# Attention and a depthwise convolution on one core: half of the last pair divided by way of DRAM, six taps moved from TensorE to VectorE

## The chip, the cores and the metric

The kernel runs on one NeuronCore of a Trainium2 chip. The metric is device time in microseconds (us) of one execution; lower is better. The time before is the median of four runs, 2910.03 us (2908.95 to 2911.59).

The engines are called by their roles: TensorE (PE in the profile) multiplies matrices, VectorE (DVE) does elementwise work, ScalarE (ACT) does activations and copies out of PSUM, GpSimd (POOL) here mostly issues DMAs, and SyncE (SP) issues DMAs only. Each engine runs its own instructions strictly in the order in which they were written.

## The reference

The input x has 16 images of 384 channels and 32 x 32 pixels, in float32. Two layers follow, each with a residual:

```python
# layer 0: attention over the 1024 pixels, 8 heads of 48 channels
x = x + _L0_conv_ref(_gn(x), L0_conv_w_qkv, L0_conv_w_proj, L0_conv_b_proj)
# layer 1: 7x7 depthwise convolution, one symmetrised filter for each channel
x = x + _L1_conv_ref(_gn(x), L1_conv_weight)
```

`_gn` is a group normalisation over 32 groups of 12 channels. Inside the attention, softmax(q k / sqrt(48)) v is computed for each head and then projected. In the convolution each output pixel is a sum over 49 taps (dy, dx), each of them one weight per channel times the shifted image.

## The kernel before, in words

Channels lie on the partitions: an image is three tiles of 128 channels x 1024 pixels. Below, "image 15" is the last of the images 0 to 15, and "tile (14, 2)" is the third channel tile of image 14.

**Attention.** The eight heads of an image are worked on as four pairs, numbered u = 4b + p. The work of a pair has two halves of 512 query columns; each half is one group of eight steps. In a group TensorE first makes eight blocks of scores (`s_step`, L493), ScalarE exponentiates them (L501), and TensorE then multiplies by v into one PSUM accumulator (`av_step`, L509). ScalarE copies the accumulator into the half `h` of `os_[u]` (`take`, L520). One extra column of v is all ones, so row 48 (and 112 for the second head) of `os_[u]` holds the sum of the exponentials, by which the rest has to be divided.

**Division by way of DRAM.** For all pairs but the last, SP copies the two rows of sums to DRAM (L527) and reads them back spread over 128 partitions (L528); VectorE takes 128 x 16 reciprocals (L534); SP writes them to DRAM (L536) and reads them back broadcast over 64 partitions for each head (L539, twice 256 KB); VectorE multiplies `os_[u]` by them (L545). These are `sums_out`, `invert` and `divide`.

**Division at once.** The last pair, u = 63, is divided half by half in `divide_at_once`: TensorE multiplies by a matrix that copies the row of sums to all rows (L588), VectorE takes the reciprocal of 128 x 512 values out of PSUM (L590) and multiplies (L591). Half 0 is divided in the last group, between its scores and its products with v; half 1 after them, in `fast_finish`. The projection of image 15 (`proj_part`, L599) runs around them: pairs 0 and 1, then pair 2, then pair 3.

**Convolution.** Most taps are one VectorE instruction each (`conv_tap`, L640): the image times a weight of its channel, added to the accumulating tile `x1s`. Taps with dx = 0 of some tiles are made on ScalarE (`product`, L621) and added by accumulating DMAs from POOL (L945). Three tiles are convolved on TensorE (`PE_TILES`): (14, 2) first, then (15, 2) and (15, 1). For them the normalised tile `xn1s` is written to DRAM (L715) and read back as shifted copies `sh` (L722, 8 DMAs of 160 KB for each half of the tile); the multiplications (`conv_on_pe`, L756) group four rows dy as one of two values d0, so that a tile has 14 products (d0, dx) for each half, of 8 instructions each. `pe_taps` (L736) leaves (1, 0) out for tile (14, 2): its dy = 1, 2, 3 with dx = 0 come from ScalarE. A half of a tile frees the buffers of its shifted copies for the next half to be loaded. The products of (14, 2) are queued in `x1_chains` and are run at the end, some of them between the small matrix products (`ps_st_x`, L332) that give the statistics of image 15.

**Order.** The program order is written by a planner in the kernel. `clock` is its estimate of TensorE's time and `vclock` of VectorE's. `after(wait, cost, f)` queues a job that is written on VectorE once `vclock` has passed the waiting time, at the cost given; `catch_up` fills VectorE with taps up to `clock`. A tap is worth about 1.0 to 1.2 us to the planner. In `x1_chains` of image 14, `vclock` is set back by 5.0 us, which leaves room for five us of taps more.

**Queues.** SP's DMAs are issued in order, and one that waits holds up all behind it: those of the division, the writes `xd` and the loads `sh`. POOL's queue holds the loads and the stores of images, the accumulating additions and the six copies (`qk_rest`, L458) that collect the last pair's q and k.

Of the kernel before, what the change touches and what calls it, by code (L numbers as in the profile page):

```python
# [10 lines left out]
F32 = mybir.dt.float32  # L11
I32 = mybir.dt.int32
AF = mybir.ActivationFunctionType
ALU = mybir.AluOpType
AX = mybir.AxisListType

P = 128
# [27 lines left out]
def kernel(  # L45
# [25 lines left out]
    nc = tc.nc  # L71

    B, C, H, W = x.shape
    N = H * W
    NK = C // P
    D = C // HEADS
    NP = HEADS // 2
    NT = N // P
    HALF = N // 2
    KS = w_conv.shape[2]  # L80
    PAD = KS // 2
    SCALE = D ** (-0.5)
    U = NP * B
    PER = C // GROUPS
    SC = 2 * N // P
# [24 lines left out]
    def run(general):  # L110
        tag = "g" if general else "f"
        with ExitStack() as stack:
# [13 lines left out]
            tpool = pool("tpool", 2)  # L126
            small = pool("small", 2)
# [16 lines left out]

            BESIDE = None if general else (B - 2, 0)
            ROWS_ONLY[BESIDE] = range(-PAD, PAD + 1)

            def taps_of(b, k):
                return [t for t in TAPS if t[1] or t[0] not in ROWS_ONLY.get((b, k), ())]
# [373 lines left out]
            def sums_out(u):  # L523
                sum_d = ddram.tile([2, N], F32, tag="sum", name=f"sum_{u}")
                for j in range(2):
                    r = 64 * j + D
                    nc.sync.dma_start(sum_d[j : j + 1, :], os_[u][r : r + 1, :])  # L527
                nc.sync.dma_start(sums[:, u, :], sum_d.rearrange("j (p c) -> (j p) c", c=SC))  # L528
# [56 lines left out]
            def divide_at_once(u, h):  # L585
                half = os_[u][:, h * HALF : (h + 1) * HALF]
                ps = ps_o.tile([P, HALF], F32, tag="acc", name=f"ps_sum_{u}_{h}")
                nc.tensor.matmul(ps, lhsT=late["masks"][:, 7, :], rhs=half, start=True, stop=True)  # L588
                inv = tpool.tile([P, N], F32, tag="t", name=f"inv_{u}_{h}")[:, 0:HALF]
                nc.vector.reciprocal(inv, ps)  # L590
                nc.vector.tensor_tensor(half, half, inv, ALU.mult)  # L591

            def proj_part(b, o, ts):
                if o not in pps:
                    pps[o] = psum(f"ps_proj_{b}_{o}")
                for t in ts:
                    lhsT = wp[:, t, o * P : (o + 1) * P] if t < NK else late["w3"][:, o * P : (o + 1) * P]
                    for h in range(2):
                        nc.tensor.matmul(  # L599
                            pps[o][:, h, :],  # L600
                            lhsT=lhsT,
                            rhs=os_[NP * b + t][:, h * HALF : (h + 1) * HALF],
                            start=(t == 0),
                            stop=(t == NP - 1),
                        )
# [128 lines left out]
            PE_TAPS.sort(key=lambda t: t[1] != 0)  # L734

            def pe_taps(b, k):  # L736
                return [t for t in PE_TAPS if t != (1, 0) or (b, k) not in ROWS_ONLY]

            def conv_on_pe(b, k, h, first, last):
                if (b, k) == PE_TILES[-1]:  # L740
# [131 lines left out]
            def after(wait, cost, f):  # L872

                nonlocal count
                count += 1
                heapq.heappush(later, (now() + wait, count, cost, f))
# [208 lines left out]
            def x1_chains(b, st):  # L1085
                nonlocal vclock
                on_pe = [t for t in PE_TILES if t[0] == b]
                for k in range(NK - 1, -1, -1):
                    conv_begin(st, b, k, nc.vector if (b, k) == (B - 1, NK - 1) else None)
                    if (b, k) in on_pe:  # L1090
                        conv_store(b, k)

                        cuts = (0, KS - 2, KS, KS + 2) if b == B - 2 else (0, KS)
                        cuts = (*cuts, len(pe_taps(b, k)))
                        pe_conv.extend((b, k, 0, *c) for c in zip(cuts, cuts[1:]))
                        pe_conv.extend(((b, k, 1, 0, KS), (b, k, 1, KS, cuts[-1])))
                if b == B - 1:
                    lone_sums(*LONE)
                    after(2.5, 0.0, lambda: lone_rows(*LONE))
                if b == B - 2:  # L1100

                    vclock -= 5.0
                    for k in range(NK):
                        spare[B - 1, k] = new_xn1(B - 1, k)
                    beside, first = BESIDE, PE_TILES[0]
                    early = [(beside, 0), (beside, -1), (beside, 1), (first, 1), (beside, -2)]
                    early += [(first, 2), (beside, 2), (first, 3), (beside, -3), (beside, 3)]
                    for n, (bk, dy) in enumerate(early):
                        applies.append(
                            (  # L1110
                                clock + 2.0 + 7.0 * n,
                                1.3,
                                lambda n=n, bk=bk, dy=dy: rows_early(*bk, n, dy),
                            )
                        )
                after(
                    2.0 if b == B - 1 else 6.0,
                    0.0,
                    lambda: chains.extend(
                        (b, k) for k in range(NK) if (b, k) not in on_pe  # L1120
                    ),
                )
# [28 lines left out]
            waiting = set()  # L1151

            def finish(u):
                sums_out(u)
                if u < U - 1:
                    waiting.add(u)
                    after(6.0 if u % NP == NP - 1 else 9.0, 0.3, lambda: finish2(u))

# [135 lines left out]

            def fast_end(b):
                assert not applies
                for key in ("sum2", "sum3"):
                    late[key] = opool.tile([P, N], F32, tag="o", name=key)
                nc.gpsimd.memset(late["sum3"][:, N - W :], 0.0)

                x1_stats[b].groups_on_pe(late["masks"], tap, conv_piece)
                conv_piece()
                x1_chains(b, x1_stats[b])
# [7 lines left out]
            for b, n0, size in [  # L1311
# [14 lines left out]
                ending = b == B - 1 and r + size == PER_B  # L1326
                if ending:
                    catch_up(clock)
                    divide_at_once(NP * b + NP - 1, 0)
                    vclock += 4.2  # L1330
                    for o in range(NK):
                        proj_part(b, o, (0, 1))
                    loads(1)
                    clock += 2 * US_PROJ
                else:
                    catch_up(clock)
                    act_slot(4.5)
                    other(n0 + size, False)
                for n in range(n0, n0 + size):
                    av_step(n)  # L1340
                    u, h, i = n // (2 * NT), n // NT % 2, n % NT
                    if i == NT - 1:
                        take(u, h)
                clock += (size * US_STEP + US_TURN) / 2
                if n0 // (2 * NT) < (n0 + size) // (2 * NT):
                    finish((n0 + size) // (2 * NT) - 1)
                if ending:
                    catch_up(clock)
                    assert not invs and not waiting
                    fast_finish(b)  # L1350
                else:
                    other(n0 + size, True)
# [91 lines left out]
```

## Time and profile before

| what | us |
|---|---|
| median of the runs | 2910.03 |
| the profiled execution's own time | 2906.77 |
| its span, first to last instruction | 2904.6 |
| TensorE busy | 2894.6 (100%) |
| VectorE busy | 2566.1 (88%) |
| ScalarE busy | 1461.5 (50%) |
| GpSimd busy | 262.2 (9%) |

The time of an engine is counted from the span's start. In a line of the timeline, the first number is the start, the second the duration of the merged run of like instructions, then come engine, source line, operation, output and inputs, shape and the number of instructions; brackets hold the idle time of the engine before them and what ended it. SPq and POOL rows of DMAs tell when the DMA was issued, not when it landed. A matmul of float32 data shows as two instructions.

### The profile page before, as it was taken

The numbers are of one execution on the slowest core, as the hardware profiler recorded it, in microseconds if no ns is written. First come the engines' busy times: TensorE is split into PE (matmuls) and PEld (weight loads), VectorE is DVE, ScalarE is ACT, GpSimd is POOL, SyncE is SP. The second block draws the span as 40 slices with busy tenths as digits, with TensorE's granted clock in tenths as the row PEclk, the third lists the DMA queues.
The fourth block names the chain that finished last, engine by engine and source line by source line (L and its number), as shares of the span: only waits on it lengthen the run. The fifth ranks groups of instructions, "written<-read, shape, count | busy, mean of one in ns | idle before, by whom it ended". The sixth has DMA issues, their size and how long they took to land.

```text
span 2904.6 us, 30161 instructions
## 1 busy us (share of the span) xinstructions
PE 2894.6 (100%) x11446; PEld 1168.4 (40%) x11446; DVE 2566.1 (88%) x2559; ACT 1461.5 (50%) x1745; POOL 262.2 (9%) x411
## 2 busy tenths in 40 slices
PE   9999999999999999999999999999999999999999
PEld 4343343433434343343433434343343433434333
DVE  5313999989899898998989899898998989899997
ACT  3546445464453645545465454645545455454641
POOL 3111004010100101000010100101001010100101
PEclk9999999999999999999999999999999999999999
DMA  7423012220312203022120212213012130222346
GB/s 287 131 26 63 16 36 77 39 66 22 66 33 43 70 21 84 16 35 70 35 71 16 64 41 43 64 28 84 16 36 70 28 77 16 53 52 43 83 125 174
DMA packets 74284, 175.80 MB, mean 61 GB/s; under 512 B 30528, under 2 KB 32464, under 8 KB 72592
## 3 DMA queue, kind: packets, MB, share of 16 engines
q0 software_dynamic: 34336, 114.90, 15.9%
q1 hardware_dynamic: 38080, 55.20, 7.5%
q10 hardware_dynamic: 1712, 3.67, 0.4%
q8 instruction: 92, 1.51, 0.2%
q14 instruction: 64, 0.52, 0.1%
HBM read 118.61 MB, written 28.72 MB: 51 GB/s over the span
## 4 chain that ended last, share of the span: by engine, by line
PE 100%; DVE 0%; ACT 0%; POOL 0%; issue 0%; POOLq 0%
PE ps_s L493 31%; PE acc L509 31%; PE ps_qk L442 17%; PE ps_v L468 9%; PE ps_proj L562 8%; PE ps_conv L756 2%; PE ps_proj L599 1%; PE warm L1182 0%; PE ps_st_x L332 0%; PE ps_sum L588 0%; ACT qk L449 0%; POOL sc_x L353 0%; DVE x L360 0%; DVE x L777 0%; DVE ones_warm L1176 0%
## 5 line engine op out<-in xcount | busy, mean ns | idle before, releaser
L640 DVE SCALAR_TENSOR_TENSOR x<-xn,wsym,x 128x930 f32<-128x930 f32 (+9 forms) x2170 | 2362.9, 1165 | 137.2 <-ACT xn L364 137.1
L501 ACT ACTIVATE e<-ps_s 128x1024 f32<-128x1024 f32 x1024 | 952.4, 1053 | 52.4 <-PE ps_s L493 49.4
L493 PE MATMUL ps_s<-qk 48*128 48x512 f32 x4096 | 914.9, 596 | 1.1 <-ACT qk L449 1.1
L509 PE MATMUL acc<-e,v 128*64 128x512 f32 x4096 | 907.2, 595 | 0.0
L493 PEld LDWEIGHTS ps_s<-qk 48*128 48x128 f32 x4096 | 375.7, 185 | 536.5 <-ACT e L501 259.9
L509 PEld LDWEIGHTS acc<-e,v 128*64 128x64 f32 x4096 | 283.0, 137 | 608.2 <-issue 601.6
L442 PE MATMUL ps_qk<-x,wqk 128*128 128x512 f32 x1152 | 505.7, 595 | 1.0 <-DVE x L360 1.0
L520 ACT COPY o<-acc 128x512 f32<-128x512 f32 x128 | 75.0, 586 | 595.9 <-PE acc L509 595.9
L442 PEld LDWEIGHTS ps_qk<-x,wqk 128*128 128x128 f32 x1152 | 216.2, 190 | 287.1 <-issue 285.7
L468 PE MATMUL ps_v<-wv,x 128*128 128x384 f32 x768 | 252.0, 488 | 0.0
L562 PE MATMUL ps_proj<-o,wp 128*128 128x512 f32 x540 | 234.2, 592 | 0.0
L449 ACT COPY qk<-ps_qk 128x1024 f32<-128x1024 f32 x96 | 96.8, 1009 | 256.3 <-PE ps_qk L442 256.3
L577 POOL DMA_DIRECT2D x<-in_x x45 | 39.3, 872 | 1802.2 <-ACT x L570 1427.8
L468 PEld LDWEIGHTS ps_v<-wv,x 128*128 128x128 f32 x768 | 144.6, 190 | 109.7 <-ACT e L501 12.1
L562 PEld LDWEIGHTS ps_proj<-o,wp 128*128 128x128 f32 x540 | 102.6, 190 | 126.0 <-issue 119.6
L477 ACT COPY v<-ps_v 128x384 f32<-128x384 f32 x128 | 55.1, 483 | 185.6 <-PE ps_v L468 185.6
L570 ACT ACTIVATE x<-ps_proj,bp 128x1024 f32<-128x1024 f32 x45 | 50.1, 1113 | 182.7 <-PE ps_proj L562 182.7
L545 DVE TENSOR_TENSOR o<-o,inv 128x1024 f32<-128x1024 f32 x63 | 77.0, 1222 | 56.6 <-DMA inv<-inv 46.7
L364 ACT ACTIVATE xn<-x,sc_x 128x1024 f32<-128x1024 f32 x47 | 54.9, 1230 | 68.8 <-DMA sc_x<-gr_x 59.5
L387 DVE BATCH_NORM_STATS2 bs_all<-xs 128x6 f32<-128x512 f32 x84 | 52.3, 683 | 19.4 <-DMA xs<-in_x 19.2
L756 PE MATMUL ps_conv<-sh,mat 128*32 128x464 f32 (+3 forms) x656 | 67.4, 569 | 0.0
L364 ACT ACTIVATE x<-x,x_sc 128x1024 f32<-128x1024 f32 x42 | 51.1, 1263 | 22.2 <-DMA x<-in_x 22.2
(143 smaller groups left out, 560.6 us busy)
## 6 DMA issues: line engine op xcount, KB each, us to landing
x<-in_x POOLq DMA_DIRECT2D x90, 512.0 KB, 5.5
inv<-inv SPq DMA_DIRECT2D x126, 256.0 KB
out<-x POOLq DMA_DIRECT2D x45, 512.0 KB, 3.8
xs<-in_x POOLq DMA_DIRECT2D x42, 512.0 KB, 6.5
qk<-qk POOLq DMA_DIRECT2D x96, 128.0 KB, 5.9
o<-o SPq DMA_DIRECT2D x90, 64.0 KB
sh<-xd SPq DMA_DIRECT2D x32, 160.0 KB
x<-in_x SPq DMA_DIRECT2D x6, 512.0 KB
```

What stands on the lines that cost most here:

```text
L364: nc.scalar.activation(dst, src, AF.Identity, bias=self.sc[:, k, 1:2], scale=self.sc[:, k, 0:1],)
L442: nc.tensor.matmul(ps[:, h, :], lhsT=wqk[:, k, s, t, :], rhs=xns[b][:, k, h * HALF : (h + 1) * HALF], start=(k == 0), stop=(k == NK - 1),)
L449: nc.scalar.copy(halves(qks[u][:, s, :]), ps)
L468: nc.tensor.matmul(ps[:, j, 0:C], lhsT=xns[b][:, k, t * P : (t + 1) * P], rhs=wv[:, k, :], start=(k == 0), stop=(k == NK - 1),)
L493: nc.tensor.matmul(ps[:, j, :], lhsT=qks[u][r, 1, i * P : (i + 1) * P], rhs=qks[u][r, 0, h * HALF : (h + 1) * HALF], start=True, stop=True,)
L501: nc.scalar.activation(es[n], ps, AF.Exp, scale=SCALE)
L509: nc.tensor.matmul(accs[u, h][64 * j : 64 * j + 64, :], lhsT=v_of(u, i, j), rhs=e[:, j, :], start=(i == 0), stop=(i == NT - 1),)
L520: nc.scalar.copy(os_[u][:, h * HALF : (h + 1) * HALF], accs.pop((u, h)))
L545: nc.vector.tensor_tensor(os_[u], os_[u], invs.pop(u), ALU.mult)
L562: nc.tensor.matmul(ps[:, h, :], lhsT=wp[:, t, o * P : (o + 1) * P], rhs=os_[NP * b + t][:, h * HALF : (h + 1) * HALF], start=(t == 0), sto ...
L640: nc.vector.scalar_tensor_tensor(acc, xn1s[b, k].rearrange("p (h w) -> p h w", w=W)[:, iy, ix], wsym[:, k, dy + PAD, dx + PAD : dx + PAD + 1],
L756: nc.tensor.matmul(dst[CH * i : CH * (i + 1), :].rearrange("p (y x) -> p y x", x=W)[:, :, ox], lhsT=mats[k][:, i, d0 * KS + dx + PAD, :], ...
```

## The change

The change has four parts.

1. Half 0 of the last pair (u = 63) is divided by way of DRAM instead of at once. `half_sums` is called when half 0 has been taken, at the end of the group before the last; `half_invert` (128 x 8 reciprocals) is written 4.0 us later and `half_divide` 7.5 us after that. Half 1 is still divided at once. SP's six DMAs of this stand in its queue at two places: the three of `half_sums` ahead of L536 and L539 of pair 62, the three of `half_invert` behind four loads `sh` and ahead of the next four.
2. The planner's 4.2 us for the division at once are gone, and `sums_out` of the last pair, which only feeds the check of the sums, is written later, in `fast_end`.
3. For tile (14, 2), `pe_taps` leaves out (1, -1) and (1, 1) besides (1, 0): 11 products for each half are left of 13. The six taps dy = 1, 2, 3 with dx = -1 and 1 become six VectorE instructions, written together 1.0 us after `x1_chains` of image 14 (`aside`), at a planned cost of 7.0 us.
4. `vclock` is set back by 3.0 us instead of 5.0, and two of ScalarE's products change places, so that the first addition to tile (14, 2) comes one place later.

```diff
+            ASIDE = (1, -1)
...
+            def half_sums(u):
+                sum_d = ddram.tile([2, HALF], F32, tag="sumh", name=f"sumh_{u}")
+                for j in range(2):
+                    r = 64 * j + D
+                    nc.sync.dma_start(sum_d[j : j + 1, :], os_[u][r : r + 1, 0:HALF])
+                late["sumh"] = small.tile([P, SC // 2], F32, tag="sumh", name=f"sumh_{u}")
+                nc.sync.dma_start(late["sumh"], sum_d.rearrange("j (p c) -> (j p) c", c=SC // 2))
+                after(4.0, 0.3, lambda: half_invert(u))
+
+            def half_invert(u):
+                nc.vector.reciprocal(late["sumh"], late["sumh"])
+                inv_d = ddram.tile([2, HALF], F32, tag="invh", name=f"invh_{u}")
+                nc.sync.dma_start(inv_d.rearrange("j (p c) -> (j p) c", c=SC // 2), late["sumh"])
+                inv = tpool.tile([P, N], F32, tag="t", name=f"invh_{u}")[:, 0:HALF]
+                for j in range(2):
+                    nc.sync.dma_start(
+                        inv[64 * j : 64 * j + 64, :], inv_d[j : j + 1, :].to_broadcast([64, HALF])
+                    )
+                after(7.5, 0.7, lambda: half_divide(u, inv))
+
+            def half_divide(u, inv):
+                half = os_[u][:, 0:HALF]
+                nc.vector.tensor_tensor(half, half, inv, ALU.mult)
+                late["half"] = True
...
             def pe_taps(b, k):
-                return [t for t in PE_TAPS if t != (1, 0) or (b, k) not in ROWS_ONLY]
+                return [t for t in PE_TAPS if (b, k) not in ROWS_ONLY or not t[0] or t[1] not in (0, *ASIDE)]
...
-                    vclock -= 5.0
+                    vclock -= 3.0
...
+                    def aside():
+                        for dy in range(1, PAD + 1):
+                            for dx in ASIDE:
+                                conv_tap(*first, dy, dx)
+
+                    after(1.0, 7.0, aside)
-                    early = [(beside, 0), (beside, -1), (beside, 1), (first, 1), (beside, -2)]
+                    early = [(beside, 0), (beside, -1), (beside, 1), (beside, -2), (first, 1)]
...
             def finish(u):
-                sums_out(u)
                 if u < U - 1:
+                    sums_out(u)
                     waiting.add(u)
...
             def fast_end(b):
                 assert not applies
+                sums_out(U - 1)
...
                     catch_up(clock)
-                    divide_at_once(NP * b + NP - 1, 0)
-                    vclock += 4.2
                     for o in range(NK):
                         proj_part(b, o, (0, 1))
...
+                if b == B - 1 and r + 2 * size == PER_B:
+                    half_sums(n0 // (2 * NT))
...
-                    assert not invs and not waiting
+                    assert not invs and not waiting and late["half"]
```

## The prediction

> **What bounds the kernel now.** I read the page first, then the chain that ended last over the tail, then the timelines of VectorE, SP and POOL over the last 200 us, and last the trace's records of when DMAs landed.
>
> ```profile
> PE 100%; DVE 0%; ACT 0%; POOL 0%; issue 0%; POOLq 0%
> ...
> 2797.64 1.05 PE ps_sum L588 x2
> ...
> 2817.93 0.86 PE ps_sum L588 x2
> ...
> 2836.95 61.22 PE ps_conv L756 x596
> 2898.17 0.02 issue
> 2898.19 0.69 DVE x L777
> ```
>
> The chain is TensorE from end to end: what leaves it could be worth its full time. But VectorE has almost no slack. In its last 200 us, but for the small steps of image 15's statistics and the very last addition, it waits only where a bracket stands here:
>
> ```profile
> 2732.14 1.23 DVE L545 TENSOR_TENSOR o<-o,inv 128x1024 f32<-128x1024 f32 x1 [0.63 <-issue]
> ...
> 2771.95 1.23 DVE L545 TENSOR_TENSOR o<-o,inv 128x1024 f32<-128x1024 f32 x1 [2.29 <-ACT xn L621]
> ...
> 2799.50 1.22 DVE L545 TENSOR_TENSOR o<-o,inv 128x1024 f32<-128x1024 f32 x1
> 2800.63 3.35 DVE L590 RECIPROCAL inv<-ps_sum 128x512 f32<-128x512 f32 x1
> 2804.09 0.69 DVE L591 TENSOR_TENSOR o<-o,inv 128x512 f32<-128x512 f32 x1
> 2804.70 12.79 DVE L640 SCALAR_TENSOR_TENSOR x<-xn,wsym,x 128x841 f32<-128x841 f32 x12
> 2817.41 1.22 DVE L901 TENSOR_TENSOR x<-x,xn 128x1024 f32<-128x1024 f32 x1
> 2818.82 3.36 DVE L590 RECIPROCAL inv<-ps_sum 128x512 f32<-128x512 f32 x1 [0.20 <-PE ps_sum L588]
> ...
> 2891.19 1.23 DVE L918 TENSOR_TENSOR sum<-sum,sum 128x1024 f32<-128x1024 f32 x1 [1.81 <-DMA sum<-tap_-3_13772]
> ```
>
> See that VectorE reaches the second reciprocal 0.20 us before TensorE's sum is there. From it a chain runs without a gap through the residual, the statistics (the mean is ready at 2831.8, as TensorE's filling piece of convolution ends at 2831.82), the normalised tiles (2839.2), their store and the loads of shifted copies. So VectorE's lateness at 2818.82, called s below, shifts the rest of the kernel by s. The 2.29 us at 2771.95 were spent on a division's DMAs: the trace has inv<-inv of pair 61 land at 2771.42 (ScalarE, which the bracket names, has no part in this multiplication). The first two queues:
>
> ```profile
> 2711.68 0.53 POOL L651 DMA_DIRECT2D out<-x  x1 [0.45 <-DVE x L640]
> 2717.37 0.87 POOL L945 DMA_DIRECT2D xn<-xn  x1 [5.16 <-ACT xn L621]
> 2717.93 2.27 POOL L458 DMA_DIRECT2D qk<-qk  x4
> ...
> 2722.18 0.34 SPq L536 DMA_DIRECT2D inv<-rec  x1
> 2727.24 1.12 SPq L539 DMA_DIRECT2D inv<-inv  x2
> ...
> 2759.71 0.34 SPq L536 DMA_DIRECT2D inv<-rec  x1
> 2761.18 1.62 SPq L539 DMA_DIRECT2D inv<-inv  x2
> ```
>
> The same 8 KB take 1.4 us at 2759.71 and 5.0 us at 2722.18, where POOL's copies are under way (their last lands at 2727.03).
>
> **Part 1, TensorE's share.** One matmul of sums (1.05 us in the chain) and, of tile (14, 2), two products for each of two halves go. The 82 such products of the three tiles (13 x 2 and 14 x 4) take 4.25 + 1.72 + 61.22 = 67.2 us, 0.82 us each; four are 3.3 us. If all were paid: -4.35 us. Neither is paid in full.
>
> The matmul at 2797.64 is followed by a wait for VectorE's second division. Counting VectorE's new order with each tap at its step between starts in the trace (1.00 us for 841 pixels to 1.16 for 992): with 128x8 reciprocals (0.16) and one multiplication (0.61) in place of 3.46 + 0.61, but four taps (4.3) more between the two divisions and L901 (1.14) moved behind the second, VectorE reaches the second reciprocal at 2818.81 if no DMA delays it, the same instant as before. The 1.05 us become idle time: 0.
>
> The 3.3 us lie where TensorE does (14, 2) while (15, 2) is normalised, stored and loaded:
>
> ```profile
> 2836.89 15.57 PE L756 MATMUL ps_conv<-sh,mat 128*32 128x464 f32 x152
> ...
> 2842.33 11.55 SPq L722 DMA_DIRECT2D sh<-xd  x6
> ```
>
> The first loads of (15, 2) go out at 2842.33, 0.07 us after the store of that tile has landed (2842.26), and land between 2845.6 and 2850.45; TensorE came to (15, 2) at 2852.33, so 1.9 us of slack. Ready 3.3 us sooner, it would wait 1.4 us. One store of an image (out, 512 KB, issued at 2847.56) moves out of this stretch with VectorE's later taps, for which I take 0.3 us. Paid: **-2.2 us** (bounds: -1.5, were the loads slower, to -3.3, were they not awaited).
>
> **Part 2, VectorE's six taps.** Two each of 961, 930 and 899 pixels: 2 x (1.13 + 1.10 + 1.07) = 6.6 us, at 2707.3. The planner's room of 7.0 + (3.0 - 5.0) puts as many other taps behind the next reciprocals: all divisions of pairs 60, 61 and 62 keep their place in VectorE's order, +0.1 us. But the last taps of image 13 move by 6.6 us, and with them its three stores on POOL, from 2709.67-2711.68 to about 2716.3-2718.3. Behind them in POOL's queue stand the addition (2717.37) and the copies qk<-qk. The stores' data took 4.3 us before, so the copies end about 2.9 us later, at 2730. The 8 KB of pair 60 then land at 2730 instead of 2727.2, the two inv<-inv after them (4.7 us from issue to landing before) at about 2735, and VectorE, there at 2731.6, is about 3 us late. (Bounds 0.6, were the stores to drain in the shadow of the addition, to 5.)
>
> That lateness puts pair 61's reciprocal from 2759.44 to 2762.5, behind the additions and loads of POOL at 2759.47 to 2762.8, which it preceded before. Its 8 KB then take some 5 us as at 2722.18, to 2768, and inv<-inv some 6.5 (10.2 before, but most of the loads have gone by then): 2774.7 instead of 2771.42. VectorE resumes about 3.2 us late; the old 2.29 us of idle time swallow the rest. Nothing after it gives this time back: **s = +3.2 us** (bounds 0 to 5).
>
> On the DMA engines, the Trainium skill (DMA: Bandwidth & Descriptors, section Queues, rings and completion order) says that an engine goes round among the queues at the bounds of packets of some 9 to 17 descriptors. By that SP's 8 KB would wait for one packet and not for all that POOL has queued, s would be about 0 and the kernel 2 us faster. The row at 2722.18 disagrees: no packet of SP's queue moved until 2725, when POOL's had drained. I go by the row.
>
> **Part 3, the half by way of DRAM.** The half is taken at 2791.20. Sums to DRAM and back: 1.2 to 2.0 us and 1.5 us in the rows of other pairs when nothing else moves: landed at 2794.5; VectorE asks at 2797.6. But pair 62's inv<-rec is queued behind these three and goes out at 2793.4 instead of 2789.91, its inv<-inv lands at 2799.9-2800.4 (5.3 us as before, with loads sh beside it), and VectorE wants it at 2800.0: 0 to 0.5 us. Then four loads sh (1.8 us of issue), the half's inv<-rec (to 2802.3-2803.2, behind those loads), its broadcast (a 256 KB one took 3.2 to 3.7 us in quiet, at 2649; the half is 128 KB each): 2806.0-2807.0, wanted at 2805.45. Alone this makes s = 0.6 to 1.6. With part 2's 3.2 us VectorE comes at 2808.7, after them: they don't add, s is the larger of the two. If every hop were as slow as the slowest rows, the broadcast would land at 2813.8: s = 8.4.
>
> **What is moved without cost.** `sums_out` of pair 63 waits for half 1's division, about 2823, and is read by the check at 2844. ScalarE's products keep their slots; the additions that now follow each other on one tile wait for each other on POOL (4 to 5 us), with 12 us to the next. VectorE's remaining taps after the second division are 3.3 us more; its last sum starts at 2893.2 + s, free of the old wait of 1.81 us, and its last tap work ends at 2895.5 + s, TensorE at 2898.17 - 2.2 + s: 0.5 us of slack left, where before it waited 3.98 us.
>
> **Sum.** -2.2 + 0 + 3.2 = +1.0 us on the profiled execution's 2906.77 us: 2907.8. That execution is 3.3 us below the median; I add the same to the median: 2910.03 + 1.0 = **2911.0 us**.
>
> **The rivals.**
> A. The queues take up the moved stores, and only part 3's wait is left: s = 1.1, -2.2 + 1.1 = -1.1, 2908.9. For it: VectorE's order of divisions hardly moves. Against it: 2722.18, where SP's small transfer waited for POOL's.
> B. TensorE's saving comes through: 4.35 us less, 2905.7. It needs the shifted copies 1.4 us earlier and VectorE 1 us ahead, and VectorE has 0.20.
> C. Slower: SP's queue. Six small dependent transfers and four loads stand one behind another between 2791 and 2807, and VectorE, all TensorE's last projection and the statistics stand behind the last. With every hop at its slowest row s = 8.4: -2.2 + 8.4 = +6.2, 2916.2. It decides from s = 2.2 on, and exceeds 0.2% from s = 8.0. Against it: nothing of POOL's is in flight then (its last addition landed at 2787.56).
>
> **Chances.** 0.2% is 5.8 us, about what a measurement of this kernel can tell from no change. Forecast 0.52 (s from 1.5 to 5: 2909.3 to 2912.8), A 0.27, B 0.08, C 0.13. The forecast, A and B lie within 0.2%; I give faster 0.04 (half of B, were more than the counted work to go), slower 0.12 (most of C), same 0.84. The range leaves out B and the upper part of C and adds 1 us for the spread of the runs: 2907.0 to 2914.5.
>
> **What would show it.** Right: the multiplication of pair 60 starts at about 2735 and that of 61 at about 2775 after 2 to 3 us of idle time each; stores of image 13 at 2716 to 2718; TensorE idle some 4 us ahead of the last projection and 1 us ahead of (15, 2), no longer 100% of the chain; the half's multiplication without a wait. Wrong: pair 61 resumed at 2772 (then A), the half's multiplication preceded by several us of idle time (C), or a span under 2901 (B).

## The result, and the profile after

The changed kernel takes 2912.75 us (median of 40 runs, 2909.41 to 2916.03), the kernel before 2909.06 us (60 runs, 2906.34 to 2913.95). The ratio is 1.0013, with an interval from 1.0009 to 1.0018: a real loss of 3.7 us, below the 0.2% that the prediction set as its bound. The profiled execution took 2912.7 us (span 2910.9), about the median.

Ahead of everything else: which work bounds the kernel. On the page after, the shares of the chain that ended last by engine read

```profile
PE 82%; DVE 12%; DMA 3%; issue 2%; ACT 0%; POOL 0%; SPq 0%; ACTq 0%; DVEq 0%; POOLq 0%
```

where it was TensorE at 100% before. VectorE and DMAs (those of the divisions and the loads of shifted copies) are now part of what ends last. The timeline of the changed kernel shows where (columns: start in us, busy time in us, engine, line, operation; in brackets the idle time ahead of it). VectorE first, then TensorE:

```profile
2723.44 0.25 DVE L536 RECIPROCAL rec<-sums 128x16 f32<-128x16 f32 x1
...
2738.74 1.23 DVE L547 TENSOR_TENSOR o<-o,inv 128x1024 f32<-128x1024 f32 x1 [5.67 <-ACT e L503]
2777.72 1.23 DVE L547 TENSOR_TENSOR o<-o,inv 128x1024 f32<-128x1024 f32 x1 [1.80 <-issue]
...
2811.08 0.68 DVE L618 TENSOR_TENSOR o<-o,invh 128x512 f32<-128x512 f32 x1
...
2824.42 3.35 DVE L592 RECIPROCAL inv<-ps_sum 128x512 f32<-128x512 f32 x1
...
2791.16 7.14 PE L495 MATMUL ps_s<-qk 48*128 48x512 f32 x32
...
2821.85 1.02 PE L627 MATMUL ps_proj<-o,mat 128*128 128x512 f32 x2
2828.62 6.91 PE L627 MATMUL ps_proj<-o,mat 128*128 128x512 f32 x10 [5.75 <-DVE o L593]
...
2844.73 12.24 PE L784 MATMUL ps_conv<-sh,mat 128*32 128x464 f32 x120
...
2858.69 45.87 PE L784 MATMUL ps_conv<-sh,mat 128*32 128x512 f32 x444 [0.82 <-DMA sh<-xd]
```

The same two places of TensorE in the kernel before:

```profile
2790.50 7.14 PE L493 MATMUL ps_s<-qk 48*128 48x512 f32 x32
...
2822.06 5.52 PE L599 MATMUL ps_proj<-o,mat 128*128 128x512 f32 x12
```

(The brackets name what came last by the profile; what VectorE waits for at both multiplications is the inv<-inv. That of pair 60 landed at 2738.56.) The multiplications of pairs 60 and 61 come 6.6 and 5.8 us later than before, and the second reciprocal 5.6 us, without a wait for TensorE. TensorE stands idle for 5.75 us ahead of the last projection. And its ten matmuls then take 6.91 us, where twelve took 5.52 before: that was in no step of the prediction. The half's multiplication (L618) waits for nothing.

The profiled executions differ by some 3 us already ahead of the last group, as is told below ("The clock at the start"). So from here on all is counted from the start of the last group's first scores (the last 32 matmuls of L493 before, of L495 after): 2790.50 before, 2791.16 after. "Late" means later than before on that count. The rows are the start of the multiplications of pairs 60 and 61, of the second reciprocal (its lateness is s), and of the very last addition (2898.19 before, 2904.60 after; its lateness is the change in the kernel's end), and for TensorE the idle time ahead of the last projection's ten matmuls and their duration. The first column is the median less that of the kernel before on the same chip; the ratio is not the quotient of these medians. One execution of half_recips took 6200.54 us and is left out of its row.

| kernel | median | ratio, interval | 60 late | 61 late | s | idle | ten matmuls | end late |
|---|---|---|---|---|---|---|---|---|
| after | +3.7 | 1.0013, 1.0009 to 1.0018 | 5.9 | 5.1 | 4.9 | 5.75 | 6.91 | 5.8 |
| half_only | +0.9 | 1.0004, 0.9995 to 1.0013 | 0.0 | 0.0 | 1.0 | 1.83 | 4.56 | 1.1 |
| stores_later | +3.9 | 1.0012, 1.0003 to 1.0021 | 4.9 | 4.3 | 4.1 | 4.93 | 6.25 | 4.3 |
| products_later | +1.5 | 1.0005, 0.9996 to 1.0014 | 0.5 | 2.8 | 2.6 | 3.40 | 5.97 | 2.7 |
| both_later | +2.0 | 1.0004, 0.9995 to 1.0013 | 0.2 | 3.0 | 2.9 | 3.68 | 7.60 | 4.3 |
| taps_later | +1.3 | 1.0004, 0.9995 to 1.0013 | 0.7 | 2.7 | 2.6 | 3.38 | 6.25 | 2.6 |
| recips_after | +4.6 | 1.0011, 1.0002 to 1.0020 | 5.6 | 2.6 | 4.7 | 5.48 | 6.08 | 4.8 |
| recips_before | -0.3 | 0.9997, 0.9988 to 1.0006 | -0.1 | -4.7 | 0.0 | none | 5.5 for twelve | 0.5 |
| recips_6 | -2.8 | 0.9987, 0.9979 to 0.9996 | 0.1 | -5.0 | -0.9 | none | 5.5 for twelve | -2.3 |
| recips_6s | -3.0 | 0.9990, 0.9981 to 0.9999 | -1.1 | -5.0 | -0.9 | none | 5.5 for twelve | -2.3 |
| half_recips | -0.7 | 0.9998, 0.9989 to 1.0006 | 0.0 | -4.6 | -0.9 | none | 5.5 for twelve | -0.8 |
| busy | +1.9 | 1.0005, 0.9996 to 1.0014 | 3.3 | 3.0 | 2.8 | filled | 5.3 for twelve | 3.1 |
| busy4 | +2.2 | 1.0007, 0.9998 to 1.0016 | 5.3 | 3.8 | 3.7 | 1.04 | 4.56 | 1.9 |

In every row with an idle time the end can be split into three parts: s, plus what the ten matmuls take beyond 4.56 us, less what TensorE's four dropped products pay. The last is what remains of the sum, not a row of its own: for the changed kernel 4.94 + 2.35 - 5.75 leaves 1.54 us paid. By the same sum the other kernels with these products gone give 1.3 to 1.8 us, and half_only, which keeps them, gives -0.1. Each row but its first two columns is one profiled execution. recips_before, whose s is 0, ends 0.5 us late, so differences of half a microsecond in the last column say little.

### The profile page after: what moved, and what is told of

It reads as the page before. It is cut to its first block, busy times and chain, and to the rows that moved or that the text cites. A ratio compares the mean times of both kernels' runs of the same rounds, so it can differ in the third digit from the quotient of the medians.

```text
span 2910.9 us, 30112 instructions
## 1 busy us (share of the span) xinstructions
PE 2895.4 (99%) x11412; PEld 1174.1 (40%) x11412; DVE 2569.9 (88%) x2565; ACT 1462.2 (50%) x1745; POOL 262.8 (9%) x411
## 4 chain that ended last, share of the span: by engine, by line
PE 82%; DVE 12%; DMA 3%; issue 2%; ACT 0%; POOL 0%; SPq 0%; ACTq 0%; DVEq 0%; POOLq 0%
PE ps_s L495 26%; PE acc L511 25%; PE ps_qk L444 15%; DVE x L668 11%; PE ps_v L470 8%; PE ps_proj L564 7%; PE ps_conv L784 2%; DMA inv<-inv 1%; DMA inv<-rec 1%; DVE o L547 0%; PE warm L1217 0%; DMA sh<-xd 0%; PE ps_proj L627 0%; PE ps_st_x L334 0%; DMA qk<-qk 0%
## 5 line engine op out<-in xcount | busy, mean ns | idle before, releaser
L668 DVE SCALAR_TENSOR_TENSOR x<-xn,wsym,x 128x899 f32<-128x899 f32 (+9 forms) x2176 | 2370.1, 1165 | 137.7 <-ACT xn L366 137.6
L495 PE MATMUL ps_s<-qk 48*128 48x512 f32 x4096 | 914.2, 596 | 1.1 <-ACT qk L451 1.1
L495 PEld LDWEIGHTS ps_s<-qk 48*128 48x128 f32 x4096 | 376.5, 185 | 535.0 <-ACT e L503 257.2
```

The costliest lines, as they stand in the source:

```text
L495: nc.tensor.matmul(ps[:, j, :], lhsT=qks[u][r, 1, i * P : (i + 1) * P], rhs=qks[u][r, 0, h * HALF : (h + 1) * HALF], start=True, stop=True,)
L668: nc.vector.scalar_tensor_tensor(acc, xn1s[b, k].rearrange("p (h w) -> p h w", w=W)[:, iy, ix], wsym[:, k, dy + PAD, dx + PAD : dx + PAD + 1],
```

## Experiments on the half that goes by way of DRAM

**half_only.** TensorE keeps its six taps; only the half is divided by way of DRAM.

```diff
-return [t for t in PE_TAPS if (b, k) not in ROWS_ONLY or not t[0] or t[1] not in (0, *ASIDE)]
+return [t for t in PE_TAPS if t != (1, 0) or (b, k) not in ROWS_ONLY]
...
-vclock -= 3.0
+vclock -= 5.0
...
-after(1.0, 7.0, aside)
-early = [(beside, 0), (beside, -1), (beside, 1), (beside, -2), (first, 1)]
+early = [(beside, 0), (beside, -1), (beside, 1), (first, 1), (beside, -2)]
```

> The first change alone: half 0 of the last pair by way of DRAM, all taps and the planner's 5.0 us as before. Theory 1 (VectorE's lateness in the changed kernel comes from the division of pair 60, held up behind POOL's late stores and copies): here VectorE reaches the division of pair 60 and of pair 61 as before (multiplications at about 2732 and 2772), and only the half's own chain costs: a wait of 0.5 to 1.6 us before one of its multiplications, TensorE idle 1 to 2.5 us ahead of the last projection, granted clock 1.0; ratio 1.0002 to 1.0006. Theory 2 (the DMA chain of the half is what makes VectorE late): the same lateness as in the changed kernel, second reciprocal at about 2824, ratio about 1.0015.

Its timeline on VectorE, and the last projection on TensorE:

```profile
2808.00 0.69 DVE L618 TENSOR_TENSOR o<-o,invh 128x512 f32<-128x512 f32 x1 [1.26 <-DMA invh<-invh]
...
2825.81 4.56 PE L627 MATMUL ps_proj<-o,mat 128*128 128x512 f32 x10 [1.83 <-DVE o L593]
```

Pairs 60 and 61 are where they were before, and s is 1.03 us, all of it the half's own wait. So part 3 alone costs about 1 us, as forecast (0.6 to 1.6), and saves nothing: the matmul of sums that went has turned into idle time. In the changed kernel the same broadcast landed at 2808.90, and VectorE, late for other reasons, wanted it at 2811.08. The two latenesses don't add.

## Experiments on the lateness of pair 60

The prediction blamed image 13's three stores on POOL. These are the rows of the changed kernel's queues and of ScalarE, from the same timeline:

```profile
2717.37 1.15 ACT L649 ACTIVATE xn<-xn,wsym 128x1024 f32<-128x1024 f32 x1 [6.43 <-DVE x L668]
2718.42 0.99 ACT L451 COPY qk<-ps_qk 128x1024 f32<-128x1024 f32 x1
2719.32 1.12 ACT L649 ACTIVATE xn<-xn,wsym 128x992 f32<-128x992 f32 x1
...
2719.58 0.53 POOL L679 DMA_DIRECT2D out<-x  x1 [0.45 <-DVE x L668]
2720.74 0.87 POOL L973 DMA_DIRECT2D xn<-xn  x1 [0.62 <-ACT xn L649]
2721.30 3.23 POOL L460 DMA_DIRECT2D qk<-qk  x6
2730.64 0.92 POOL L973 DMA_DIRECT2D xn<-xn  x1 [6.11 <-ACT xn L649]
...
2723.71 0.34 SPq L538 DMA_DIRECT2D inv<-rec  x1
2731.41 1.43 SPq L541 DMA_DIRECT2D inv<-inv  x2
```

The late stores are there (the last at 2719.58). But a second waiter is there too, which the prediction had not looked for. ScalarE's first product (L649) writes a buffer that VectorE's last taps of image 13 still read, and waits 6.43 us for them. Behind it on ScalarE stand a copy of qk and the second product (2719.32). Only the end of that one lets POOL's addition (L973) go, and the addition stands ahead of the copies qk<-qk.

**stores_later** moves the stores alone to behind the copies:

```diff
+elif b == B - 3:
+    after(24.0, 0.0, lambda: conv_end(b, k))
 else:
     conv_end(b, k)
```

> The changed kernel with only POOL's order changed: the three stores of image 13 are issued behind the copies of q and k and three additions instead of ahead of them; VectorE, TensorE, ScalarE and SP are instruction for instruction the same. Theory 1: the copies no longer wait for 1.5 MB of stores; they still start some 3 us late, since ScalarE waits for VectorE's end of image 13 first. Reciprocals of pair 60 land some 3 us sooner than at 2731.4, its multiplication starts at 2734 to 2736 instead of 2738.7, TensorE's idle time ahead of the last projection is 2 to 4 us instead of 5.75: ratio 0.9998 to 1.0008. Theory 2 (the stores have no part in it, VectorE's own load has): no change, 1.0013.

Pair 60 is still 4.9 us late, and the median is that of the changed kernel. The cause that the prediction named falls. On its timeline ScalarE still waits for VectorE:

```profile
2718.91 1.15 ACT L649 ACTIVATE xn<-xn,wsym 128x1024 f32<-128x1024 f32 x1 [6.73 <-DVE x L668]
...
2722.28 0.95 POOL L975 DMA_DIRECT2D xn<-xn  x1 [15.97 <-ACT xn L649]
2722.85 3.29 POOL L460 DMA_DIRECT2D qk<-qk  x6
```

**products_later** and **both_later** plan ScalarE's products 8 us later, so that the first one comes behind the first copy of qk, and the first addition behind all six copies qk<-qk; the second moves the stores as well.

```diff
-clock + 2.0 + 7.0 * n,
+clock + 10.0 + 7.0 * n,
```

> The changed kernel with ScalarE's products alone planned 8 us later, image 13's stores where the change has them. Theory 1 (either wait for VectorE is enough): ScalarE copies qk at about 2715, but POOL's stores still stand ahead of the copies until 2719.6 to 2720.1, so the first copies go out at about 2720.5 and the last at 2723.5, less than 1.2 us earlier than in the changed kernel; pair 60 is 2.5 to 5 us late, s = 2.3 to 4.3, ratio 1.0005 to 1.0013. Theory 2 (only ScalarE's wait counts): the copies go out before 2718 for the most part, 60 within 1 us of before, s under 2, ratio 0.9996 to 1.0002.

> The changed kernel with image 13's three stores planned 24 us later on POOL and with ScalarE's products planned 8 us later, so that the first of them stands behind the first copy of qk. VectorE's order is that of the changed kernel. Theory 1 (the copies qk<-qk are late because VectorE's end of image 13 is awaited in two places, by ScalarE's first product and by POOL's stores, and each is enough): with both out of the way ScalarE copies qk at about 2715 again, POOL's last two copies go out at about 2722, inv<-inv of pair 60 at 2727 to 2729, its multiplication starts within 1 us of before (counted from the last group's first scores), pair 61 within 2 us, s = 0.7 to 2.0; TensorE then waits 1.5 to 2.8 us for the last projection, its clock stays at 1.0, and the tail is -1.1 to +0.2 us against before: ratio 0.9996 to 1.0002. Theory 2 (pair 60 is late for another reason, such as VectorE's own order or the transfers beside it): 60 stays 3 us or more late, s 2.8 or more, ratio 1.0008 to 1.0014.

With either, pair 60 is back within 0.5 us. Of products_later:

```profile
2714.41 1.01 ACT L451 COPY qk<-ps_qk 128x1024 f32<-128x1024 f32 x1 [4.74 <-PE ps_qk L444]
...
2718.62 0.53 POOL L679 DMA_DIRECT2D out<-x  x1 [0.45 <-DVE x L668]
2719.17 2.91 POOL L460 DMA_DIRECT2D qk<-qk  x6
...
2722.76 0.34 SPq L538 DMA_DIRECT2D inv<-rec  x1
2726.95 1.12 SPq L541 DMA_DIRECT2D inv<-inv  x2
...
2774.11 1.22 DVE L547 TENSOR_TENSOR o<-o,inv 128x1024 f32<-128x1024 f32 x1 [4.90 <-issue]
```

The stores are as late as in the changed kernel, the copies go out only some 1 us earlier on the common count, as the first theory said; but the last of them lands 2.9 us earlier (at 2726.73; in the changed kernel at 2730.94), the 8 KB of inv<-rec take 4.2 us instead of 7.7, and pair 60 is in time, as the second said. So the products' place decides, and the stores' does not.

Products and additions moved together, but the rows speak for the addition. In the changed kernel ScalarE's copy of qk has ended at 2719.41, and POOL's copies go out at 2721.30, right behind the addition. And where some 1 us is in the issue, the other 2 us are in the time to landing, with no addition of 0.5 MB ahead of the copies in POOL's queue. By the trace the 8 KB wait for the copies' data: in twelve of the fourteen profiles inv<-inv goes out 0.1 to 0.5 us after the last copy qk<-qk has landed. In the other two (busy and recips_6s) it goes out 0.9 to 1.0 us before.

Neither kernel reached the 0.9996 to 1.0002 that goes with pair 60 in time: pair 61 is 3 us late in both, since the moved products also moved POOL's additions, one of which now goes out 1.4 to 1.7 us ahead of pair 61's inv<-rec. That took 2.8 and 3.1 us instead of 1.5, and the inv<-inv behind it fell behind all of POOL's loads.

## Experiments on pair 61

**taps_later** plans the six taps 7 us later, behind image 13's end.

```diff
-after(1.0, 7.0, aside)
+after(8.0, 7.0, aside)
```

> The changed kernel with one number changed: the six taps are written 8.0 us after x1_chains of image 14 instead of 1.0, behind the end of image 13 on VectorE; every queue keeps its order. Theory 1: stores of image 13 go out at about 2710 to 2712 as before, the reciprocals of pair 60 reach DRAM in 5 us, its multiplication starts at about 2733 with under 1.5 us of idle time, the second reciprocal within 1.5 us of its time before, TensorE idle 1 to 2.5 us with the clock at 1.0; TensorE then gets its 2 us from the fewer products: ratio 0.9993 to 1.0000. Theory 2 (VectorE simply has more work than the planner left room for): as the changed kernel, ratio about 1.0013.

Pair 60 is back, as expected, but not pair 61: the ratio missed the expected 0.9993 to 1.0000, and TensorE waited 3.38 us, with its clock halved, where 1 to 2.5 us at full clock were expected.

```profile
2761.52 0.85 POOL L973 DMA_DIRECT2D xn<-xn  x1 [9.56 <-ACT xn L649]
2762.06 1.19 POOL L973 DMA_DIRECT2D x<-xn  x1
2762.60 2.29 POOL L1412 DMA_DIRECT2D x<-in_x  x3
...
2762.84 0.24 DVE L536 RECIPROCAL rec<-sums 128x16 f32<-128x16 f32 x1
...
2763.11 0.34 SPq L538 DMA_DIRECT2D inv<-rec  x1
2769.65 1.09 SPq L541 DMA_DIRECT2D inv<-inv  x2
...
2776.74 1.23 DVE L547 TENSOR_TENSOR o<-o,inv 128x1024 f32<-128x1024 f32 x1 [3.68 <-issue]
```

The reciprocal is only 1.35 us late, but that puts it behind POOL's additions and loads. Its 8 KB then take 6.5 us, where they took 1.5 in front of them. This is the second half of the prediction's part 2, now by itself.

**recips_6** keeps taps_later's edit and plans the reciprocals of pairs 61 and 62 after 6 instead of 9 us. **recips_6s** also plans the six taps one by one, 2.2 us apart, between taps of other tiles. **recips_after** and **recips_before** have the early reciprocals alone, in the changed kernel and in the kernel before.

```diff
-after(6.0 if u % NP == NP - 1 else 9.0, 0.3, lambda: finish2(u))
+after(6.0 if u % NP == NP - 1 or u > U - NP else 9.0, 0.3, lambda: finish2(u))
```

recips_6s has this on top:

```diff
+n = 0
 for dy in range(1, PAD + 1):
     for dx in ASIDE:
-        conv_tap(*first, dy, dx)
+        after(2.2 * n, 1.15, lambda dy=dy, dx=dx: conv_tap(*first, dy, dx))
+        n += 1
...
-after(8.0, 7.0, aside)
+after(8.0, 0.0, aside)
```

> As the last try with early reciprocals and later taps, but the six taps in a row on one tile as the change has them. Theory 1 (a row of dependent taps costs VectorE 0.7 us more, but VectorE had 1.4 us to spare at the second reciprocal): each of the six steps 0.10 to 0.13 us longer than a tap between other tiles, the wait for TensorE's sum shrinks from 1.43 to 0.5 to 0.9 us, the tail as there: -1.9 to -2.6 us, ratio 0.9988 to 0.9994. Theory 2 (7 us of taps in a row push pair 60 or 61 behind POOL's transfers again): s of 1 us or more, ratio 0.9998 to 1.0006.

> The changed kernel with the six taps planned 7 us later and one by one, 2.2 us apart, between taps of other tiles, and with the reciprocals of image 15's pairs 61 and 62 planned 6 instead of 9 us after their sums. Theory 1 (s comes from pair 60 by way of the late end of image 13, from pair 61 by a reciprocal that falls behind POOL's additions and loads, and 0.7 us from six taps in a row on one tile): 60 within 0.8 us of before, the reciprocal of 61 ahead of POOL's additions at 2759 and its multiplication within 1 us of before, s = 0 to 1.3; TensorE waits under 2.3 us for the last projection at a clock of 1.0, and the tail is -1.8 to -0.5 us against before, ratio 0.9994 to 1.0000. Theory 2 (the moved DMAs of pair 62 now stand ahead of the half's sums and make the half's multiplication wait in place of them): 2 to 3 us of idle time ahead of the half's multiplication, s = 2 to 3.5, ratio 1.0001 to 1.0008.

> The changed kernel with these two reciprocals planned 6 instead of 9 us, the six taps where the change has them. Theory 1 (pair 60's lateness puts every later division back, so both places have to be mended): pair 60's multiplication stays 3 to 6 us late, the reciprocal of 61 comes 1.5 to 3 us after POOL's additions instead of 5, inv<-rec still takes over 4 us, s = 1.5 to 4, and TensorE waits 2 to 4.5 us for the last projection with its clock halved for at least one stretch: ratio 1.0003 to 1.0012. Theory 2 (the early reciprocals alone bring pair 61 back): 61 at most 1 us late, s under 1, no clock loss, ratio 0.9990 to 0.9998.

> The kernel before, with the reciprocals of image 15's pairs 61 and 62 planned 6 instead of 9 us after their sums, and nothing else. Theory 1 (TensorE is the bound there from end to end, and VectorE only meets it at the second reciprocal): pair 61's multiplication comes 4 to 5 us earlier than before (counted from the last group's first scores), VectorE waits 1 to 3 us for TensorE's second sum, and the tail stays within 0.3 us: ratio 0.9996 to 1.0004. Theory 2 (the earlier reciprocals are what made the last try fast, with or without the change): tail 1.5 to 3 us shorter, ratio 0.9990 to 0.9995.

The timeline of recips_6:

```profile
2759.58 0.26 DVE L536 RECIPROCAL rec<-sums 128x16 f32<-128x16 f32 x1
...
2769.64 1.23 DVE L547 TENSOR_TENSOR o<-o,inv 128x1024 f32<-128x1024 f32 x1
...
2820.64 3.36 DVE L592 RECIPROCAL inv<-ps_sum 128x512 f32<-128x512 f32 x1 [0.82 <-PE ps_sum L590]
...
2823.87 5.54 PE L627 MATMUL ps_proj<-o,mat 128*128 128x512 f32 x12
...
2852.62 7.94 PE L784 MATMUL ps_conv<-sh,mat 128*32 128x512 f32 x76 [0.87 <-DMA sh<-xd]
```

Pair 61's division has no wait at all; even the 2.29 us that the kernel before spent there are gone. VectorE is then in front: it waits for TensorE's second sum, which itself comes a matmul of sums earlier (s = -0.86). The last projection runs in one piece, and the end comes 2.3 us earlier. Both kernels have intervals below 1: 2.8 and 3.0 us faster than before, 0.1%, the best found here. recips_6s was faster than expected (an end 1.8 to 0.5 us earlier, a ratio of 0.9994 to 1.0000).

Both places have to be mended. In recips_after, pair 60 is still 5.6 us late and drags pair 61's reciprocal (2764.66, its inv<-rec taking 7.0 us) behind POOL's loads (2761.56 to 2764.9); s is 4.7 and TensorE's idle time 5.48 us, above the 1.5 to 4 and the 2 to 4.5 expected. (Two of its eleven executions took 2904.3 and 2908.3 us, the others 2910.7 to 2916.0. What went differently in these two is not known; neither was profiled.) And the early reciprocals are nothing by themselves: in recips_before VectorE's wait for TensorE's second sum only grows from 0.20 to 2.09 us, with a ratio of 0.9997.

**half_recips** is half_only with the same edit to the reciprocals.

> The half by way of DRAM alone (TensorE keeps the six taps), with the two early reciprocals. Theory 1 (the matmul of sums is worth its 1.05 us as soon as VectorE comes early enough, and the rest of the gain with early reciprocals is TensorE's share of the taps): no wait of TensorE ahead of the last projection, the second reciprocal 0.6 to 1.1 us earlier than before, the tail -1.1 to -0.5 us, ratio 0.9993 to 0.9999. Theory 2 (the half's chain is late even so, behind pair 62's DMAs): a wait over 1 us ahead of the half's multiplication, tail 0 or later, ratio 1.0000 to 1.0006.

The second reciprocal comes 0.85 us earlier, the end 0.8: the matmul of sums is worth most of its microsecond once VectorE comes early enough. The median (-0.7) is too close to 0 to be told from it. Against recips_6, whose end is 1.5 us earlier still, this leaves 1.5 us for TensorE's share of the taps, as the sum under the table does.

## Experiments on the slow matmuls

The averages over stretches of the changed kernel (columns: stretch, its length, then the busy time of PE, PEld, DVE, ACT and POOL, the granted clock, the DMA share and GB/s):

```profile
2824.00:2826.00 2.00, 0.00 (x0) 0.00 (x0) 2.00 (x2) 0.00 (x0) 0.00 (x0) 1.00 0.00 0
2826.00:2828.00 2.00, 0.00 (x0) 0.00 (x0) 1.90 (x2) 0.00 (x0) 0.00 (x0) 0.64 0.00 0
2828.00:2830.00 2.00, 1.38 (x2) 0.84 (x3) 2.00 (x3) 0.00 (x0) 0.00 (x0) 0.50 0.01 4
2830.00:2832.00 2.00, 2.00 (x3) 0.67 (x2) 1.88 (x2) 0.00 (x0) 0.00 (x0) 0.50 0.04 4
2832.00:2834.00 2.00, 2.00 (x4) 0.86 (x3) 0.16 (x2) 1.89 (x4) 0.00 (x0) 0.65 0.04 8
2834.00:2836.00 2.00, 2.00 (x12) 0.62 (x14) 1.97 (x3) 0.80 (x3) 0.00 (x0) 1.00 0.00 0
```

The clock falls to 0.5 in the idle time and stays there for most of the projection. **busy** and **busy4** fill the idle time with matmuls of 128x512 whose result nothing reads: seven in the first, four in the second.

```diff
+busy = ps_o.tile([P, HALF], F32, tag="acc", name="busy")
+for _ in range(7):
+    nc.tensor.matmul(
+        busy,
+        lhsT=late["masks"][:, 7, :],
+        rhs=os_[NP * b][:, 0:HALF],
+        start=True,
+        stop=True,
+    )
 for o in range(NK):
     proj_part(b, o, (NP - 1,))
```

> The changed kernel with seven matmuls of no use (12 instructions' worth of about 6 us, results never read) put on TensorE between the products of pair 2 and of pair 3, where it waits 5.75 us. Theory 1 (the wait costs twice: itself, and the granted clock, which falls to 0.5 after it and makes the next ten matmuls take 6.9 us instead of 4.6): the clock stays at 1.0, the ten matmuls take 4.6 us, the chain from there is 2.1 us shorter, ratio 1.0004 to 1.0008. Rival (the clock's fall is not what lengthens it: the matmuls wait for VectorE's residuals): the same length of the chain, ratio 1.0013 or more.

> The changed kernel with four matmuls of 128x512 that serve nothing (eight instructions, some 3.4 us) ahead of the last projection, half as long as the filling tried before, so that they end before VectorE's division does. Theory 1 (the last projection's matmuls are slow because TensorE stood idle for 5.75 us and its clock was halved): the idle time left is under 2.5 us, the clock stays at 1.0, the ten matmuls of the projection take 4.6 us instead of 6.9, and the tail is s - 1.8 us against before, with s between 2.8 and 5 by what the transfers do: +1.0 to +3.2, ratio 1.0004 to 1.0010, some 2 us under the changed kernel at the same s. Theory 2 (they are slow for another reason, such as their operands): still 6 us or more, tail as in the changed kernel at the same s, ratio 1.0011 to 1.0016.

busy kept the clock at 1.0, but its filling ended some 1.4 us after VectorE's division did, which ate part of the gain. busy4 shows it clean:

```profile
2822.86 3.60 PE L1322 MATMUL busy<-o,masks 128*128 128x512 f32 x8
2826.29 1.02 PE L627 MATMUL ps_proj<-o,mat 128*128 128x512 f32 x2
2828.35 4.56 PE L627 MATMUL ps_proj<-o,mat 128*128 128x512 f32 x10 [1.04 <-DVE o L593]
```

The same ten matmuls take 4.56 us, and the end is 1.9 us late with s = 3.7: 1.8 us less than s, where the changed kernel lost 0.8 more than s. The clock, not the operands, made them slow.

## Why the prediction held, and which of its steps failed

The range and the class held: 2911.0 us forecast, 2912.75 measured. The size of the change did not: it was +3.7 us where +1.0 was forecast, outside what the forecast's own chance of 0.52 stands for (s from 1.5 to 5, a change of -0.7 to +2.8). That the time still lies within 2909.3 to 2912.8, by 0.05 us, is luck: the kernel before has a median of 2909.06 in 60 runs, not the 2910.03 of the four runs.

In the profiled pair three terms were too small, all in the same direction: 0.7 us less was paid by the four products, s was 1.7 us larger, and 2.35 us of slow matmuls were missing. With the +1.0 forecast this gives the 5.75 us by which the end comes later. The working step by step:

- **Matmul of sums, 0.** Right for this kernel. half_recips shows the condition: VectorE some 1 us earlier, which the prediction had put under its rival B. Its count of VectorE's new order is slightly off: the terms listed put VectorE 0.1 us ahead at the second reciprocal and not at the same instant, and in the trace it is 0.3 us (from pair 62's multiplication 18.81 us, before 19.12).
- **Four products, -2.2.** The mechanism is right (TensorE waits for the loads of tile (15, 2)), the size is -1.5, the lower bound given. Most of the gap is in the rows: from the store of that tile to the first load behind it took 3.66 us (2847.06 to 2850.72) instead of 3.11 (2839.22 to 2842.33).
- **Pair 60, 3 us late.** The lateness is right in kind, its named cause is wrong, and its size was 5.9 on the common count. The step that failed is "with them its three stores on POOL". What waits for the moved end of image 13 and counts is ScalarE's product, with the copies of qk and an addition behind it. By that way the copies landed 3.2 us late where 2.9 were forecast: near, but by luck. The rest of the 5.9 us was not in the forecast. The inv<-inv went out 3.5 us late and then took 7.33 us to the multiplication instead of 4.90 (2731.41 to 2738.74; before 2727.24 to 2732.14), since it fell 0.8 us behind POOL's next addition (2730.64). In busy, where it went out 0.6 us ahead of that addition in the same order of work, VectorE waited 2.83 us instead of 5.67. So the size varies between executions, from 3.3 to 5.9 us in those profiled. VectorE's own reciprocal is 0.9 us late instead of 0.1, since six taps in a row on one tile cost 0.6 us more than counted; but that is no part of the 5.9 us: in products_later it is 1.2 us late, with pair 60 in time.
- **Pair 61.** Right in its mechanism. Its two transfers took 5.8 and 5.9 us (5 and 6.5 forecast), behind POOL's loads. It resumed at 2777.72 instead of 2775.2 since pair 60 was later than assumed; **s** was 4.9 instead of 3.2, within the bounds of 0 to 5 (in the profiles' own times it is 5.6).
- **Part 3, hidden behind part 2.** Right, in both directions: no wait in the changed kernel, 1.26 us alone.
- **What was missing.** An idle time of 4 us ahead of the last projection was forecast, at no cost but itself. It halved the clock, and the ten matmuls cost 2.35 us more in the profiled run.
- **The profiled execution against the median.** The 3.3 us between them in the kernel before were taken to be spread. Some 2 us of it are probably the clock at the program's start (below), since that execution had none of its halving. In the profiled pair, 5.9 us apart, the start makes only 0.7 us; the end still comes 5.8 us late on the common count, while the medians differ by 3.7. So this execution's tail seems to be longer than most: in it the clock was halved for 6.83 us at the last projection, in stores_later and recips_after for 3.41, with ends 4.3 and 4.8 us late. With one profile of each kernel this is not shown.

Of the rivals, A would have needed pair 61 resumed at 2772, and C a wait at the half's multiplication; neither is there. B's terms, in the part that the loads allow, are what recips_6 shows.

## What to carry to other kernels

Work that is put ahead of something delays everything that waits for that thing's end, on every engine: ask of each buffer who writes it next, not only of each result who stores it. A small transfer that must land in time belongs ahead of the bulk transfers of another queue; 1.35 us of lateness put it behind them here and made it take 5 us longer, so plan it with a margin. And each wait on TensorE of 3.4 us or more cost more than itself here: the clock fell with it.

## What the runs showed of the hardware

**The clock after an idle time.** Idle times of 1.04 and 1.83 us ahead of the last projection left the granted clock at 1.0; 3.38 to 5.75 us halved it, in the clock records for 3.41 us (taps_later, stores_later, products_later, recips_after) or 6.83 us (after, both_later). The Trainium skill (TensorE: Matmul & The Clock Gate, Part 1: The HAM clock gate) says that the clock drops to half after an idle window of about 3.4 us, and that the windows run freely, so that the moment of a change depends on where in a window the work begins. The runs agree in that both lengths are a whole number of such windows, and that the fall isn't tied to the idle time's start: in the changed kernel it comes at 2826.56, within the idle time (2822.87 to 2828.62), in taps_later at 2829.05, 1.4 us after the idle time (2824.26 to 2827.64) had ended. That a whole window must be idle they do not show: 3.38 and 3.40 us are a little less than one and were enough. Between 1.83 and 3.38 us no run has an idle time here.

**The clock at the start.** In some executions the clock records show the same halving between 11.7 and 20.3 us of the span. By its length (none, 3.41 or 6.83 us) the last group's scores start at 2789.9 to 2790.9, 2791.2 to 2791.9, or 2792.2 to 2793.2 us. The profiled execution of before had none of it. Comparing two profiled executions at their ends mixes this with the change; comparing them from a late common point does not.

**Taps in a row on one tile.** In the changed kernel the six taps, each of which reads the last one's result, follow each other at 1.26, 1.26, 1.22, 1.22 and 1.19 us (with 0.04 us of idle time between), where taps of these sizes take 1.13, 1.10 and 1.07 from start to start when another tile's tap follows: 0.6 us in all. VectorE's spare time at the second reciprocal differs by the same 0.6 us: 0.82 in recips_6, with the taps in a row, against 1.43 in recips_6s, with other tiles' taps between them.
